# A division six cells behind its head, a supply that counts steps without matmuls, and an output bias on VectorE

## The chip, the cores and the metric

The kernel runs on one core of a Trainium2 chip. The metric is the device time of one execution in microseconds (us), taken as the median of several runs. Engines are named as in the profile: PE is TensorE's matmul, PEld its weight load, DVE is VectorE, ACT ScalarE, POOL GpSimd, and SP (SPq for its queue) the engine that issues most of the transfers.

## The reference

Two transformer blocks run one after the other on x, which is 2 batches of 1024 rows by 256 columns in fp32. The context has 64 tokens a batch. Layer 0 ends with a mixture of 8 experts of which each row takes two; layer 1 masks part of the context and ends with a plain feed-forward part.

```python
# layer 0
q = _ln(latents, sa_ln_g, sa_ln_b)
x = latents + _mha(q, q, sa_in_w, sa_in_b, sa_out_w, sa_out_b)      # 16 heads of 16
qc = _ln(x, ca_q_ln_g, ca_q_ln_b)
kv = _ln(tokens, ca_kv_ln_g, ca_kv_ln_b)
x = x + _mha(qc, kv, ca_in_w, ca_in_b, ca_out_w, ca_out_b)
x = _fuse_moe(x, ...)      # top 2 of 8, gates by softmax, gelu(h @ fc1) @ fc2
# layer 1
x = x + softmax(q @ k.T * SCALE) @ v @ sa_proj        # on layer_norm(x)
x = x + softmax(q @ kc.T * SCALE + bias) @ vc @ ca_proj
x = x + (gelu(layer_norm(x) @ fc1_w.T + fc1_b) @ fc2_w.T + fc2_b)
```

## The kernel before

**Cells.** The self-attention of a layer is a loop over 128 cells (lines 949 to 986), 64 for each batch. Eight cells in a row belong to one group of four heads, and a cell is one of that group's 8 blocks of 128 keys. The loop works on two cells at once. For the cell itself it makes four score matmuls of 128 x 512 ("b", L807), whose exponentials ScalarE takes (L813). For the cell that is LEAD = 10 ahead it makes four score matmuls of the other orientation ("a", L796), whose maxima over the keys VectorE takes (L803). Each matmul fills one of the eight PSUM banks; they go out in two slots of four, two of each kind. So in cells 0 to 117 VectorE has four maxima a cell, and in the last ten cells none; `maxima[0]` holds which of the two is the case, and helper() (L305) returns GpSimd while maxima are made and VectorE otherwise.

**Products.** Every even cell, the weights of the two cells before are multiplied with the values (L858, eight matmuls a cell), ScalarE copies the bank to a part buffer (L870; there are two), and helper() adds it to the head's sum (L871). If an odd cell has placed little other work (`most > 2.0`, L984), its predecessor's product is issued in the odd cell alone; then the even cell behind it has only its own half.

**Maxima to queries.** When the maxima of a head group are complete, VectorE gathers them (L831) and largest(h) transposes them on PE (L704) and subtracts them from the queries (L706). This is a task that may run at the next cell, and it is forced in the one after, before the first "b" scores of that head group.

**End of a head group.** finish() (L710) runs three cells behind a group's last. For each pair of groups it sends sums by DMA, takes reciprocals one cell later (L488), spreads them through a DMA two cells later (by_s<-turns, L493), and divides the result by them with helper() at `late` cells (L499, `late = 3 + maxima[0]`). At late + 1 the output projection (L428, added to x at L436) is made a task, and with it the cross-attention of those 512 rows; in layer 0 then their dispatch to the experts (L1294), in layer 1 the normalization of the feed-forward part (L1787).

**Filler.** All work beside the cells is a task of a Stream (L131): a generator that issues some instructions and yields a cost. A positive cost is the time of PE that they take; zero or a negative one means that only other engines work and that the task should wait so long. Stream.step (L152) picks the able task that is due first and repeats until a step has a positive cost. The loop keeps a debt, `owed`, to which each cell adds Stream.pace (at least 2.5 in layer 0 and 1.1 in layer 1, more where tasks have a due cell), and in a cell calls step until the debt is under 0.6 or `most`, which begins at 3.0, is spent:

```python
            owed = min(owed, 3.0) + max(stream.pace(cell), 0.0 if has_a else 2.0)
...
            most = 3.0
            while owed > 0.6 and most > 0.0:
                cost = stream.step(cell)
                if cost is None:
                    break
                owed -= cost
                most -= cost
```

A task that yielded a zero or negative cost can't run again in the same cell. What is left when the cells end is issued by Stream.rest (L178), by rank. In layer 0 the experts' slots follow (L1644, L1674, with indirect stores on POOL's queue); in layer 1 the rest of the cross-attention and the feed-forward part (L1804, L1816).

**Cross-attention and bias.** The cross-attention of 512 rows has scores (L1101, L1131), maxima (L1151), a subtraction of them by POOL while maxima are made and else by VectorE (L1152), exponentials (L1171), sums and reciprocals (L1190, L1199) and products with a division (L1205, L1212). add_bias (L417) adds a row of 256 to x: the self-attention's output bias before the blocks of a batch are used, the cross-attention's (layer 0), and the bias of the last feed-forward matrix (layer 1, L1793). All of it ran on GpSimd (L420). Each engine works its instructions off in the order in which the program issues them.

Of the kernel before, what the change touches and what calls it, by code (L numbers as in the profile page):

```python
# [45 lines left out]
ALU = mybir.AluOpType  # L46
# [4 lines left out]
P = 128  # L51
B, S, D, H, DH = 2, 1024, 256, 16, 16
# [78 lines left out]
class Stream:  # L131


    def __init__(self, rate):
        self.tasks, self.made, self.rate = [], set(), rate

    def add(self, steps, cost, **k):
        self.tasks.append(Task(steps, cost, **k))

# [12 lines left out]
    def step(self, cell):  # L152
        while True:
            able = [t for t in self.tasks if t.first <= cell and self.made.issuperset(t.after)]
            if not able:
                return None
            cost = self.advance(min(able, key=lambda t: (t.last, -t.rank)), cell)
            if cost and cost > 0.0:
                return cost

    def pace(self, cell):

# [39 lines left out]
def two_blocks(  # L202
# [16 lines left out]
    nc = tc.nc  # L219
# [83 lines left out]
    maxima = [True]  # L303

    def helper():  # L305

        return nc.gpsimd if maxima[0] else nc.vector
# [109 lines left out]
    def add_bias(first, nt, bias):  # L417
        for t0 in range(first, first + nt, 2):
            xb = x_sb[:, t0 : t0 + 2, :]
            nc.gpsimd.tensor_tensor(xb, xb, bias.unsqueeze(1).to_broadcast([P, 2, D]), ALU.add)  # L420

    def project_task(src, w, first, t0, n):

# [45 lines left out]
    def send(o, n, half, sm):  # L469


        nc.sync.dma_start(out=sm[64 * half : 64 * (half + 1), :], in_=o[DH::32, :])
        nc.sync.dma_start(out=whole[n, P * half : P * (half + 1), :], in_=o)

    def gather(n, dst):

        nc.sync.dma_start(
            out=dst, in_=whole[n].rearrange("(h r) q -> h r q", r=32)[:, :DH, :]
        )

    def next_heads():

        npair[0] += 1
        return npair[0] - 1

    def invert(n, sm):

        nc.vector.reciprocal(sm, sm)  # L488
        nc.sync.dma_start(out=turns[n], in_=sm)

    def spread_out(n, by):

        nc.sync.dma_start(  # L493
            out=by,
            in_=turns[n].rearrange("(h c) q -> h (c q)", h=8).unsqueeze(1).to_broadcast([8, DH, 512]),
        )

    def divide(dst, by):
        helper().tensor_tensor(dst, dst, by, ALU.mult)  # L499
# [17 lines left out]
    def self_attention(layer, tail, heads, arrive, extra, when_ready, beside=None):  # L517
# [27 lines left out]
        stream, later = Stream(RATE[layer]), {}  # L545
        maxima[0] = True

        def at_cell(cell, go):
            later.setdefault(cell, []).append(go)
# [143 lines left out]
        def need_heads(h):  # L693
            if h % 2 == 0:
                if h // 4 % 2 == 0 and h > 0:
                    stream.until(("K", h))
                stream.until(("Q", h))
# [12 lines left out]
        def finish(h, cell):  # L710


            b, qh, g = h // 8, h // 4 % 2, h % 4
            if g == 0:
                ot[b, qh] = opool.tile([P, 2, 512], F32, tag="ot", name=f"ot_{names}{b}{qh}")
            if layer == 0 and h >= 8 * B - 2:

                if g == 3:
                    stream.add(
                        side_by_side([acc.pop(h - 1), acc.pop(h)], ot[b, qh][:, 1, :]), 2.0,  # L720
                        mark="compact", rank=80,
                    )
                    project(b, qh, ["compact"])
                return
            if g % 2 == 0:
                sm = small.tile([P, 32], F32, tag="sums", name=f"sums_{names}{h}")
                sums[g // 2] = next_heads(), sm
            n, sm = sums[g // 2]
            dst = ot[b, qh][:, g // 2, :]
            send(acc.pop(h), n, g % 2, sm)  # L730
            if g % 2 == 1:
                by = opool.tile([P, 512], F32, tag="by", name=f"by_{names}{h}", bufs=1)
                gather(n, dst)
                at_cell(cell + 1, lambda: invert(n, sm))
                at_cell(cell + 2, lambda: spread_out(n, by))

                late = 3 + maxima[0]
                at_cell(cell + late, lambda: divide(dst, by))
                if g == 3:
                    at_cell(cell + late + 1, lambda: project(b, qh))  # L740

        def side_by_side(parts, dst):

            i, o = bank()
            j, s = bank()
            for half, part in enumerate(parts):
                nc.tensor.matmul(
                    o[64 * half : 64 * (half + 1), :], lhsT=picks[:, O_ROWS : O_ROWS + 64],
                    rhs=part, start=True, stop=True,
                )  # L750
            for half, part in enumerate(parts):
                for c in range(4):
                    nc.tensor.matmul(
                        s[32 * c : 32 * (c + 1), :P],
                        lhsT=picks[:, O_PART + 32 * half : O_PART + 32 * (half + 1)],
                        rhs=part[:, c * P : (c + 1) * P],
                        start=(half == 0),
                        stop=(half == 1),
                    )
            inv = small.tile([P, P], F32, tag="inv", name=f"inv_{names}", bufs=1)  # L760
            nc.vector.reciprocal(inv, s[:, :P])
            nc.scalar.copy(dst, o)
            free.extend((j, i))
            yield 1.5
            yield -1.6
            i, by = bank()
            for c in range(4):
                nc.tensor.matmul(
                    by[:, c * P : (c + 1) * P],
                    lhsT=picks[:, O_HEAD + c * P : O_HEAD + (c + 1) * P],  # L770
                    rhs=inv, start=True, stop=True,
                )
            nc.vector.tensor_tensor(dst, dst, by, ALU.mult)
            free.append(i)
            yield 0.55
            yield -1.0

        def project(b, qh, after=()):
            def go():
                for t0 in range(0, 4, 2):  # L780
                    yield from project_task(ot[b, qh], w, b * TB + 4 * qh + t0, t0, 2)
                when_ready(b, qh, stream, now[0])

            stream.add(go(), 4.0, last=now[0] + 4, rank=60, after=after)
# [45 lines left out]
        def collect(h):  # L830
            nc.vector.tensor_reduce(spread[h % 2][:, :, DH::32], mx.pop(h), AX.X, ALU.max)  # L831
# [8 lines left out]
        def slot(parts):  # L840

            drains = [score(*p) for p in parts]
            for i, drain in drains[::2] + drains[1::2] if len(parts) == 4 else drains:
                drain()
                free.append(i)
# [103 lines left out]
        for cell in range(ncell + 2):  # L949
            now[0] = cell  # L950
            ahead = cell + LEAD
            if ahead < ncell and ahead % 16 == 0:
                need_heads(ahead // 8)
            has_a, has_b = ahead < ncell, cell < ncell
            maxima[0] = has_a
            a = [("a", ahead, j) for j in (2, 3, 0, 1)] if has_a else []
            s = [("b", cell, j) for j in range(4)] if has_b else []
            if has_a:
                slot(s[:2] + a[:2])
                slot(s[2:] + a[2:])  # L960
            elif has_b:
                slot(s)
            if ahead % 8 == 7 and has_a:
                h = ahead // 8
                collect(h)
                stream.add(largest(h), 0.75, first=cell + 1, last=cell + 2, mark=("QB", h))
            if (cell + 1) % 8 == 0 and cell + 1 < ncell:
                stream.until(("QB", (cell + 1) // 8))
            for go in later.pop(cell, []):
                go()  # L970
            owed = min(owed, 3.0) + max(stream.pace(cell), 0.0 if has_a else 2.0)
            if cell >= 2 and cell % 2 == 0:
                product([c for c in (cell - 2, cell - 1) if c not in alone])
                if owed < 2.5:
                    continue
# [8 lines that stand above are left out]
            if cell % 2 == 1 and most > 2.0 and cell < ncell:  # L984
                alone.add(cell - 1)
                product([cell - 1])
# [945 lines left out]
    stream, later, _, _ = block(0, tail)  # L1932
# [47 lines left out]
    with ExitStack() as tail:  # L1980
        stream, later, made, ready = block(1, tail, heads, beside)
# [155 lines left out]
```

## Time and profile before

| what | before |
|---|---|
| median of 3 runs | 1632.26 us (1632.18 to 1632.59) |
| profiled execution | 1638.78 us, span 1637.0 us, mean granted TensorE clock 0.978 |
| cells of layer 0 | 52.5 to 592.6 us |
| cells of layer 1 | 965.0 to 1474.1 us, its cell 118 at 1438.8 us |
| maxima on VectorE, L803 | 1024 of 682 ns, 634.7 us busy |
| exponentials, L813 | 1024 of 609 ns |
| addition L871 on POOL, on DVE | 141 of 1272 ns, 14 of 694 ns |
| copies L870 on ACT | 155 of 598 ns |
| division L499 on POOL | 12 of 1271 ns, 59.6 us idle before ten of them, until by_s landed |
| add_bias, L420, on POOL | 16 for output biases of 1272 ns, 8 for the last bias of 1295 ns |
| L1152 on POOL, on DVE | 38 of 1054 ns, 26 of 692 ns |

A row of groups shows the line, the engine, the operation, its tiles with their shapes, how often it ran, then busy us and the mean ns of one, then the engine's idle time before such instructions and what ended it. A row of the timeline shows the start, the duration, the engine and the operation, and in brackets the idle time before it and what it waited for. A row of the windows shows the busy time of PE, PEld, DVE, ACT and POOL in a stretch with their instructions, then the granted clock of TensorE, the share of DMA and GB/s.

### The profile page before, as it was taken

How to read it: one execution, taken by the hardware profiler on the slowest of the kernel's cores; microseconds unless marked ns; L12 is line 12 of the kernel's file. 1: busy time of each engine (PE TensorE's matmuls, PEld its weight loads, DVE VectorE, ACT ScalarE, POOL GpSimd, SP SyncE). 2: the span in 40 equal slices, each digit the busy share in tenths (PEclk: the TensorE clock that was granted, in tenths of full speed). 3: DMA queues.
4: the chain of work that ended last, by engine and by line, in shares of the span. 5: the costliest groups of instructions: out<-in, count | busy, mean ns of one | idle time of the engine just before them, and what ended most of it. 6: DMA issues, size and time to landing. Idle time of an engine off the chain costs nothing.

```text
span 1637.0 us, 28319 instructions
## 1 busy us (share of the span) xinstructions
PE 1591.4 (97%) x10710; PEld 882.4 (54%) x10710; DVE 982.7 (60%) x2094; ACT 912.9 (56%) x1767; POOL 410.6 (25%) x545
## 2 busy tenths in 40 slices
PE   7999999999999998999999999999999999999998
PEld 3433444544543446878888753344344435446766
DVE  5796767687678647421113457876867867855400
ACT  3486767676765753333322327876776676674321
POOL 2243423134235202141112032411321323321010
PEclk9898999999999998999999999999999999999999
DMA  5234311101000105276567321000110002000000
GB/s 157 111 132 171 131 27 34 28 21 47 14 21 34 53 30 188 78 270 216 176 204 241 91 65 33 21 27 17 38 39 19 25 14 83 15 14 21 14 13 26
DMA packets 55751, 121.07 MB, mean 74 GB/s; under 512 B 12218, under 2 KB 26428, under 8 KB 55228
## 3 DMA queue, kind: packets, MB, share of 16 engines
q1 hardware_dynamic: 51772, 109.07, 20.9%
q0 software_dynamic: 3456, 9.51, 1.6%
q8 instruction: 86, 1.41, 0.4%
q10 hardware_dynamic: 384, 0.66, 0.2%
q14 instruction: 53, 0.43, 0.1%
HBM read 71.68 MB, written 38.88 MB: 68 GB/s over the span
## 4 chain that ended last, share of the span: by engine, by line
PE 89%; DVE 7%; issue 1%; ACT 1%; DMA 1%; another core or an unknown queue 1%; POOL 0%; SPq 0%; DVEq 0%; POOLq 0%; ACTq 0%
PE banks L807 16%; PE banks L796 15%; PE banks L858 14%; PE banks L1674 8%; PE banks L1644 8%; PE banks L626 4%; PE banks L428 3%; PE banks L1816 3%; PE banks L1804 3%; DVE mx_s L803 3%; PE banks L1131 2%; PE banks L596 2%; PE banks L1167 2%; PE banks L360 2%; PE banks L1101 2%
## 5 line engine op out<-in xcount | busy, mean ns | idle before, releaser
L803 DVE TENSOR_REDUCE mx_s<-banks 128x1 f32<-128x512 f32 x1024 | 634.7, 682 | 221.2 <-PE banks L796 214.9
L813 ACT ACTIVATE pt_s<-banks 128x512 f32<-128x512 f32 x1024 | 532.6, 609 | 155.5 <-PE banks L796 124.4
L796 PE MATMUL banks<-KS,QS 16*128 16x512 f32 x2048 | 539.5, 633 | 4.0 <-ACT part_s L870 1.6
L807 PE MATMUL banks<-qb_s,KS 32*128 32x512 f32 x2048 | 519.2, 623 | 6.6 <-DVE qb_s L706 3.7
L871 POOL TENSOR_TENSOR acc_s<-acc_s,part_s 128x512 f32<-128x512 f32 x141 | 179.4, 1272 | 442.2 <-ACT part_s L870 441.5
L807 PEld LDWEIGHTS banks<-qb_s,KS 32*128 32x128 f32 x2048 | 181.3, 187 | 178.6 <-DVE mx_s L803 104.4
L858 PE MATMUL banks<-pt_s,v_s 128*20 128x512 f32 x2048 | 264.1, 607 | 1.5 <-DVE mx_s L803 1.0
L796 PEld LDWEIGHTS banks<-KS,QS 16*128 16x128 f32 x2048 | 201.1, 186 | 76.8 <-issue 37.3
L1674 PE MATMUL banks<-w_slot,h_s 128*128 128x256 f32 x640 | 145.4, 383 | 3.0 <-ACT h_s L1650 3.0
L858 PEld LDWEIGHTS banks<-pt_s,v_s 128*20 128x20 f32 x2048 | 43.2, 99 | 187.5 <-ACT pt_s L813 132.1
L1674 PEld LDWEIGHTS banks<-w_slot,h_s 128*128 128x128 f32 x640 | 121.7, 192 | 23.5 <-ACT h_s L1650 3.4
L870 ACT COPY part_s<-banks 128x512 f32<-128x512 f32 x155 | 92.7, 598 | 65.1 <-PE banks L858 54.5
L1683 DVE SCALAR_TENSOR_TENSOR ys<-banks,gate,b 128x256 f32<-128x256 f32 x40 | 19.3, 483 | 174.2 <-PE banks L1674 166.3
L1650 ACT ACTIVATE h_s<-banks,w_slot 128x256 f32<-128x256 f32 x104 | 43.7, 471 | 111.6 <-issue 65.3
L1689 POOL DMA_INDIRECT results<-ys,to x40 | 38.7, 967 | 255.0 <-DVE ys L1683 211.2
L1644 PE MATMUL banks<-xsT,w_slot 128*128 128x256 f32 x416 | 95.6, 381 | 0.7 <-ACT xsT L367 0.7
L1644 PEld LDWEIGHTS banks<-xsT,w_slot 128*128 128x128 f32 x416 | 77.4, 190 | 14.9 <-DVE mx_s L803 2.3
L1152 POOL TENSOR_TENSOR sc_c<-sc_c,mx_c 128x512 f32<-128x512 f32 x38 | 40.0, 1054 | 102.4 <-DVE mx_c L1151 102.4
L626 PE MATMUL banks<-xT_s,w_att 128*128 128x512 f32 x128 | 64.7, 642 | 0.0
L1807 ACT ACTIVATE h_f<-banks,w_ff 128x512 f32<-128x512 f32 x32 | 22.0, 687 | 73.9 <-PE banks L1804 73.9
L1650 ACT ACTIVATE h_s<-banks,spare 128x256 f32<-128x256 f32 x56 | 23.4, 471 | 62.8 <-issue 31.3
L1816 PE MATMUL banks<-w_ff,h_f 128*128 128x256 f32 x256 | 57.3, 380 | 0.0
(269 smaller groups left out, 1651.4 us busy)
## 6 DMA issues: line engine op xcount, KB each, us to landing
w_slot<-in_ff_w_dram SPq DMA_DIRECT2D x40, 576.0 KB
sorted_rows<-fill SPq DMA_DIRECT2D x36, 520.0 KB
w_slot<-in_ff_w_dram SPq DMA_DIRECT2D x26, 514.0 KB
whole<-acc_s SPq DMA_DIRECT2D x30, 256.0 KB
spare<-in_ff_w_dram SPq DMA_DIRECT2D x14, 514.0 KB
xs<-sorted_rows SPq DMA_DIRECT2D x20, 260.0 KB
y<-results SPq DMA_DIRECT2D x16, 256.0 KB
QS<-stq_s SPq DMA_DIRECT2D x124, 32.0 KB
```

The source lines that it names most:

```text
L626: nc.tensor.matmul(p, lhsT=w[:, at + k * D + pair * P : at + k * D + (pair + 1) * P], rhs=xT[b][:, k, blk * 512 : (blk + 1) * 512], start= ...
L796: nc.tensor.matmul(sc, lhsT=QS[h % 4][r, qc * P : (qc + 1) * P], rhs=K[r, kh * 512 : (kh + 1) * 512], start=True, stop=True,)
L803: return i, lambda: nc.vector.tensor_reduce(mx[h][:, qc, j, kh : kh + 1], sc, AX.X, ALU.max)
L807: nc.tensor.matmul(sc, lhsT=K[r, n * P : (n + 1) * P], rhs=QB[h][r, :], start=True, stop=True)
L813: nc.scalar.activation(pt, sc, AF.Exp, scale=SCALE)
L858: nc.tensor.matmul(o[32 * j : 32 * j + VW, :], lhsT=V[b][:, cell % 8, 4 * g + j, :], rhs=exps.pop((cell, j)), start=(cell == cells[0]), st ...
L870: nc.scalar.copy(part, o)
L871: helper().tensor_tensor(acc[h], acc[h], part, ALU.add)
L1644: nc.tensor.matmul(ph[:, n, :], lhsT=w[:, at : at + P], rhs=xT[:, k, :], start=(k == 0), stop=(k == 1),)
L1650: nc.scalar.activation(h1[:, f, :], ph[:, n, :], AF.Gelu, bias=w[:, W_B1 + f : W_B1 + f + 1])
L1674: nc.tensor.matmul(py, lhsT=h1[:, f, h * P : (h + 1) * P], rhs=w[:, f * D : (f + 1) * D], start=(f == 0), stop=(f == 7),)
L1816: nc.tensor.matmul(py[:, n, :], lhsT=h1[:, f, t * P : (t + 1) * P], rhs=w2[:, f * D : (f + 1) * D], start=(f == 0), stop=(f == 7),)
```

## The change

Three things are changed. A Stream has a number `others`, which the loop sets to 0.8 in the cells that make maxima and to 0 in the last ten; a step then returns at least that number as its cost, also where the step had a zero or negative cost, and so a step that issued no matmul now ends the search and is taken off both `owed` and `most`. A task's own remaining cost, from which the pace is worked out, is not touched, and Stream.rest does not use the number. Second, `late` is 6 while maxima are made and 3 otherwise, so the division stands six cells behind finish() and the projection seven. Third, add_bias uses helper() instead of GpSimd, so it is VectorE's where no maxima are made.

```diff
@@ class Stream
         self.tasks, self.made, self.rate = [], set(), rate
 
+        self.others = 0.0
+
@@ step
             cost = self.advance(min(able, key=lambda t: (t.last, -t.rank)), cell)
-            if cost and cost > 0.0:
-                return cost
+            if cost is not None and max(cost, self.others) > 0.0:
+                return max(cost, self.others)
@@ add_bias
-            nc.gpsimd.tensor_tensor(xb, xb, bias.unsqueeze(1).to_broadcast([P, 2, D]), ALU.add)
+            helper().tensor_tensor(xb, xb, bias.unsqueeze(1).to_broadcast([P, 2, D]), ALU.add)
@@ finish
-                late = 3 + maxima[0]
+                late = 6 if maxima[0] else 3
                 at_cell(cell + late, lambda: divide(dst, by))
                 if g == 3:
                     at_cell(cell + late + 1, lambda: project(b, qh))
@@ the loop over cells
             maxima[0] = has_a
+            stream.others = 0.8 if has_a else 0.0
```

## The prediction

> **What bounds the kernel now.** I read the page's totals, the groups, the chain that ended last, a table of four stretches (attention of layer 0; experts; layer 1's cells 0 to 117; the rest), the timeline around the largest gaps, then the waits.
>
> ```profile
> PE 1591.4 (97%) x10710; PEld 882.4 (54%) x10710; DVE 982.7 (60%) x2094; ACT 912.9 (56%) x1767; POOL 410.6 (25%) x545
> PE 89%; DVE 7%; issue 1%; ACT 1%; DMA 1%; another core or an unknown queue 1%; POOL 0%; SPq 0%; DVEq 0%; POOLq 0%; ACTq 0%
> L803 DVE TENSOR_REDUCE mx_s<-banks 128x1 f32<-128x512 f32 x1024 | 634.7, 682 | 221.2 <-PE banks L796 214.9
> 52.50:592.60 540.10, 532.62 (x3911) 235.99 (x3912) 390.79 (x753) 371.33 (x718) 174.02 (x227) 0.96 0.17 57
> 592.60:965.00 372.40, 359.40 (x1820) 292.20 (x1820) 146.81 (x522) 122.04 (x264) 67.38 (x70) 0.97 0.50 165
> 965.00:1438.80 473.80, 466.55 (x3638) 208.46 (x3638) 347.43 (x608) 330.82 (x632) 135.85 (x171) 0.99 0.12 34
> 1438.80:1637.00 198.20, 190.72 (x1181) 123.85 (x1180) 63.64 (x133) 74.56 (x130) 17.23 (x48) 1.00 0.05 17
> ```
>
> TensorE is the bound nearly everywhere, and the matmuls do not change. So a gain can only be stall between them or throttled clock. Columns: span, PE, PEld, DVE, ACT, POOL busy, clock. The clock is 0.96 in layer 0 and 0.99 to 1.00 in layer 1: layer 0 loses about 540 x 0.04 = 22 us to half-clock stretches, inside a busy time that looks full.
>
> I took a cell's duration less its matmuls at full speed as its stall. Layer 0's cells 0 to 117 hold 60.7 us of stall (9.5 at start-up), layer 1's 26.7 us (5.9 at start-up), 0.23 a cell. Two places in layer 0 stand out, cells 23 and 24 (7.8 us) and 111 and 112 (9.2 us):
>
> ```profile
> 135.69 1.27 POOL L499 TENSOR_TENSOR ot_s<-ot_s,by_s 128x512 f32<-128x512 f32 x1 [7.63 <-DMA by_s<-turns]
> 136.91 3.95 POOL L871 TENSOR_TENSOR acc_s<-acc_s,part_s 128x512 f32<-128x512 f32 x3
> 138.21 0.59 ACT L870 COPY part_s<-banks 128x512 f32<-128x512 f32 x1 [3.31 <-POOL acc_s L871]
> 138.84 1.70 PE L796 MATMUL banks<-KS,QS 16*128 16x512 f32 x4 [1.62 <-ACT part_s L870]
> ```
> ```profile
> 135.20:150.50 15.30, 13.68 (x53) 3.57 (x52) 5.97 (x10) 5.90 (x11) 7.54 (x6) 0.67 0.37 147
> 520.70:539.80 19.10, 17.87 (x65) 5.86 (x64) 12.77 (x27) 7.91 (x15) 10.67 (x10) 0.73 0.11 38
> ```
>
> The division L499 waits in POOL's queue for its transfer, three additions wait behind it, the copy L870 waits for a part buffer, and PE for a bank. The clock is then 0.67. At cell 111 VectorE runs the search's and normalization's small operations between maxima; the clock is 0.73.
>
> [...] The trace agrees on the half (a pair of L807 takes 1.06 us from 143 on, 0.59 before) but gaps of only 1.6 us (before 139.3) or 1.0 us (before 402) were followed by it, while four gaps of 0.90 us were not. [...] here L871 takes 1272 ns on POOL and 694 on VectorE, 1.8x.
>
> **The change, part by part.**
>
> *1. Division at +6 while maxima are made.* The matmuls, the division and its 1.27 us stay; it moves two cells, 2 x 2.93 = 5.9 us (a bare cell runs 1047.26 to 1050.19), and issues no DMA. The projection it is tied to moves too: 8 matmuls in 2 steps, with an addition L436 of 0.69 us each on VectorE. At cell 23 POOL would reach the division at cell 24, about 138, after the transfer's landing at 135.69: the 7.63 us wait goes, and with it the 7.8 us of cells 23 and 24, which include about 10.2 x 0.5 = 5.1 us of half clock. What is late next is the ordinary limit of a cell. Elsewhere the division's waits (59.6 us in all) hold only an idle POOL: nothing. Value -7.5, ends -8 and -2 (a transfer late by more cells, or half clock from another gap).
>
> *2. Steps of other engines counted at 0.8 in layer 0.* The order of the changed kernel's instructions has the same filler matmuls there (155.2 against 151.6 us by cell 126), later by 2 to 8 cells and spread: dispatch in cells 75 to 83 and 104 to 116, one step a cell, the search at 114 to 119. Addressable stall, from the cells: 44-47 0.9; 67-70 1.4; 75-80 5.8; 82-84 6.3; 97-102 2.75; 105-108 5.4; 111-112 9.2; 114-116 1.0: together 32.7. A cell has 2.93 - 2.48 = 0.45 us of VectorE to spare beside its maxima: cells 106 and 107 held 2.2 to 2.5 us of small operations and stalled 1.82 and 2.38, so one step of 1.0 us a cell leaves about 0.55. What I expect in their place: 75-81 four steps and two bare cells 3.4 to 3.8 (3.4), 108-112 the same (3.8), 69 and 99 2.0, search in 114-119 1.0, half clock again in some (half a chance of 4) 2.0, the unexplained 1 us "issue" gap of cell 83 with the half clock behind it (half a chance of 5.5) 2.75, and bare odd cells: 15.0. Bare odd cells are new: 9, 45, 57, 89 (and 75, 79, 109, 111, in the sums above) have no product and no filler: 1.93 us of matmuls (2.85 less 0.92 of a product) against 2.48 us of maxima. PE then waits for VectorE to free a bank, with the next cell's scores and so ScalarE's exponentials queued behind. The trace has no such cell; behind odd cells with some 0.5 us of filler the stall is 0.43 to 0.58 (cell 54 of layer 1: 5.56 us for 5.00). Bounds: 0.5 and 1.0 (0.5 + the missing 0.5); value 0.8, 4 x 0.8 = 3.2, so 18.2 remain. Gain 32.7 - 18.2 = 14.5, ends 4 and 24.
>
> *3. The same in layer 1.* Filler in cells 0 to 117 falls from 136.3 to 104.2 us: 32 us of matmuls, mostly cross-attention, move behind cell 118. PE-bound work moved into a PE-bound stretch costs nothing; its surroundings do. Six bare odd cells (9, 51, 77, 91, 101, 113): 6 x 0.8 = 4.8. The query maxima L704/L706 are forced at the last moment in 9 heads instead of 5; such a cell shows this wait:
>
> ```profile
> 1152.04 0.68 DVE L706 TENSOR_TENSOR qb_s<-QS,banks 128x512 f32<-128x512 f32 x1
> 1152.87 0.70 PE L807 MATMUL banks<-qb_s,KS 32*128 32x512 f32 x2 [0.90 <-DVE qb_s L706]
> ```
>
> That is stall 0.98 a cell: 4 x 0.8 = +3.2. Fewer cross steps inside cells give back 3, uneven rest +1: together +6. Ends -3 and +20 (below). In the rest, 30 us more cross work lies in a PE that is 96% busy there; its chain uses VectorE (L1152 692 ns against POOL's 1054), 12 such operations move to it in the changed order. I take +3 for holes where L1199 (958 ns) or L1152 is waited for, ends -1 and +10. The last forward part keeps about 10.4 us of matmuls as cover for the last normalization against 12: nothing.
>
> *4. Bias by VectorE without maxima.* Ten of 24 L420 (POOL 1.27 us) become VectorE's, about 0.69 us as for L871: the eight of the forward part and two behind layer 0's cells. Behind cell 118 VectorE is 32% busy (63.64 of 198.20) and matmuls fill 96%: that is the cover. Nothing; without the cover 10 x 0.69 = +7 at most, -3 if POOL's latency was waited for.
>
> *5. Queues.* The dispatch's indirect stores on POOL move with their steps, 2 to 8 cells; the SP order differs in 28 places, spreads of QS and KS. Experts begin after the cells as before. Their own holes (7.08 us at 627, 5.65 at 697, 6.54 at 720, beside weight loads) may shift: 0, ends -4 and +4. The copies L870 fall from 155 to 139 and the additions with them: POOL and ACT are not the bound, nothing.
>
> Sum: -7.5 - 14.5 + 6 + 3 = -13. Since no trace shows the bare cell and half clock comes and goes, I keep 10 of it, i.e. 3 us for throttling in new places. Profiled execution: 1638.78 (span 1637.0 and 1.8 around it), so 1628.8; the median of the runs is 6.5 lower, 1632.26, giving 1622.3.
>
> **Rivals.** *Layer 1's cells run dry (slower).* VectorE's maxima alone are 118 x 2.48 = 293 of 474 us, and taking 32 us of matmuls from those cells saves 32 only if the cells stay PE-bound; behind cell 118 the 32 us are paid in full. For: the bare cells and the late L706. Against: the mean cell keeps (474 - 32)/118 = 3.7 us, above 2.48. If the stall doubles from 0.23 a cell (+27 us) against the gain of 22 in layer 0 and +3 behind, 1632.3 + 8 = 1640. It decides from (22 - 3)/118 = 0.16 us a cell.
>
> *The stalls only move (no change).* Small VectorE operations still stand between maxima, one cell later[...]. For: half clock followed gaps as short as 0.6 to 1.0 us. Against: a step a cell is what the cell's slack of VectorE (2.93 - 2.48) can nearly hold. Layer 0 then gains only 9: 1632.3 - 9 + 9 = 1632.
>
> *Only the division acts.* -7.5 and layer 1's bare cells undone by its saved steps, +1 behind: 1626.
>
> **How the numbers follow.** Forecast 0.45 (own range 1610 to 1629), only the division 0.13, no change 0.14, slower 0.28. The measurement tells 0.2% (3.3 us) from no change: faster is below 1629.0. Faster 0.58, same 0.14, slower 0.28. The range leaves out 0.1 below (both gains at their ends, -32 + 6 + 3 less some: 1608) and 0.1 above 1642.
>
> **What would show it.** In the changed profile: no POOL wait of 7 us for by_s and no clock of 0.67 near 140; the stretch of cells 0 to 117 of layer 0 shorter by 15 to 25 us, its clock 0.98; layer 1's same cells shorter by about 26 (32 - 6), the rest longer by 33; L870 139 times; cells such as 51 and 91 at 2.5 us and more with DVE gapless. It is wrong if layer 1's cells shorten by less than 15, if layer 0's clock stays at 0.96, or if the experts' stretch differs by over 4 us.

## The result and the profile after

The changed kernel takes 1652.29 us (median of 14 runs) against 1632.42 us of before: it is slower, ratio 1.0096 with a 95% interval of 1.0081 to 1.0111, some 15.7 us. The medians lie further apart, 19.9 us, and the means 16.5 us; what follows is taken from ratios. The forecast was 1622 us, its range ended at 1642 us.

Executions of one kernel lie 3 to 21 us apart here (11 us for the kernel before, 18 for the changed one), so small effects are taken from the ratios, and the traces, each of one execution, serve for the places. The profiled execution after took 1649.77 us (span 1648.0, clock 0.981), 11.0 us above that of before. These are the page's totals, chain and clock row after:

```profile
PE 1595.4 (97%) x10710; PEld 893.1 (54%) x10710; DVE 991.2 (60%) x2128; ACT 904.8 (55%) x1743; POOL 362.6 (22%) x495
PEclk9899999999998998999999999999999999999999
PE 90%; DVE 6%; DMA 1%; issue 1%; another core or an unknown queue 1%; ACT 0%; SPq 0%; POOL 0%; DVEq 0%; POOLq 0%; ACTq 0%
```

The matmuls are the same 10710, and the kernel is as full as it was: shares do not show a loss. The four stretches that the prediction was built on do. This is the table of windows after, with layer 0's cells, the experts, layer 1's cells 0 to 117, and the rest:

```profile
51.40:588.90 537.50, 531.71 (x3893) 239.13 (x3891) 388.81 (x750) 364.08 (x703) 156.16 (x213) 0.97 0.17 57
588.90:964.00 375.10, 359.07 (x1843) 293.28 (x1840) 146.77 (x528) 118.23 (x259) 65.07 (x68) 0.98 0.49 164
964.00:1418.10 454.10, 442.44 (x3348) 192.74 (x3348) 334.56 (x582) 316.52 (x604) 115.36 (x143) 1.00 0.12 35
1418.10:1648.00 229.90, 220.60 (x1469) 146.16 (x1468) 87.66 (x191) 91.77 (x153) 10.07 (x43) 0.98 0.05 15
```

| stretch | before | after | difference | forecast |
|---|---|---|---|---|
| lead-in | 52.5 | 51.4 | -1.1 | 0 |
| layer 0's cells | 540.1 | 537.5 | -2.6 | -22 |
| experts | 372.4 | 375.1 | +2.7 | 0 |
| layer 1's cells 0 to 117 | 473.8 | 454.1 | -19.7 | -26 |
| rest of layer 1 | 198.2 | 229.9 | +31.7 | +33 |

The two large numbers of layer 1 came near the forecast, but together they are +12.0 instead of the +9 of the prediction's sum (its terms, 32 us moved and 3 of stall, would make the last row +35), and layer 0's gain is missing almost whole. Cells 0 to 117 of layer 0 alone are 7.6 us shorter (505.6 to 498.0), 6.8 of it less loss by clock, but cells 118 to 127 are 4.8 us longer. The first place to look at is the division at cell 23. This is the timeline after, at the same place as before (L501 is the division, L873 the addition, L872 the copy, L798 a score):

```profile
136.72 1.27 POOL L501 TENSOR_TENSOR ot_s<-ot_s,by_s 128x512 f32<-128x512 f32 x1 [7.52 <-DMA by_s<-turns]
137.94 3.95 POOL L873 TENSOR_TENSOR acc_s<-acc_s,part_s 128x512 f32<-128x512 f32 x3
139.23 0.58 ACT L872 COPY part_s<-banks 128x512 f32<-128x512 f32 x1 [3.20 <-POOL acc_s L873]
139.87 1.13 PE L798 MATMUL banks<-KS,QS 16*128 16x512 f32 x4 [1.51 <-ACT part_s L872]
```

The wait has not moved: 7.52 us, three additions behind it, a copy, a gap on PE. (The half clock behind it took 3.4 us in this execution, from 141.1 on, and 10.2 us in that of before.) The division is issued two cells later in the program, yet POOL takes it up where it did before. The kernel writes the order out by hand for PE, DVE, ACT and SP only (the `manual_schedule` in its head); POOL's order is left to the framework's scheduler, and in both traces the division stands behind the same two additions of the next head group. The sentence ahead of the prediction, that each engine works in the order of the program, is wrong for POOL. The prediction used the changed kernel's order of instructions, but placed the division in POOL's queue as the program issues it.

For what follows, time was split in each trace into idle time of PE (no matmul on it), loss by clock (duration times 1 less the granted clock) and the remainder. Here "half clock" is a stretch at a granted clock of 0.5; in all traces such stretches last a multiple of 3.41 us (3.41 to 13.65 in that of before), unless the execution ends in them. Since a trace is one execution, the loss by clock was also averaged over all executions of a kernel, each of which has its span and mean clock on record; that table stands behind the experiments.

### The profile page after: what moved, and what is told of

The parts are those of the page before. It is cut to its first block, busy times and chain, and to the rows that moved or that the text cites. A ratio compares the mean times of both kernels' runs of the same rounds, so it can differ in the third digit from the quotient of the medians.

```text
span 1648.0 us, 28264 instructions
## 1 busy us (share of the span) xinstructions
PE 1595.4 (97%) x10710; PEld 893.1 (54%) x10710; DVE 991.2 (60%) x2128; ACT 904.8 (55%) x1743; POOL 362.6 (22%) x495
## 4 chain that ended last, share of the span: by engine, by line
PE 90%; DVE 6%; DMA 1%; issue 1%; another core or an unknown queue 1%; ACT 0%; SPq 0%; POOL 0%; DVEq 0%; POOLq 0%; ACTq 0%
PE banks L809 17%; PE banks L798 15%; PE banks L860 14%; PE banks L1677 8%; PE banks L1647 8%; PE banks L628 4%; PE banks L430 3%; PE banks L1807 3%; PE banks L1819 3%; DVE mx_s L805 2%; PE banks L1134 2%; PE banks L598 2%; PE banks L1170 2%; PE banks L1104 2%; PE banks L362 1%
## 5 line engine op out<-in xcount | busy, mean ns | idle before, releaser
L798 PE MATMUL banks<-KS,QS 16*128 16x512 f32 x2048 | 537.9, 629 | 2.4 <-ACT part_s L872 1.5
L809 PE MATMUL banks<-qb_s,KS 32*128 32x512 f32 x2048 | 525.5, 620 | 13.0 <-DVE qb_s L708 7.3
L809 PEld LDWEIGHTS banks<-qb_s,KS 32*128 32x128 f32 x2048 | 187.0, 186 | 184.9 <-DVE mx_s L805 105.4
L873 POOL TENSOR_TENSOR acc_s<-acc_s,part_s 128x512 f32<-128x512 f32 x127 | 160.9, 1267 | 433.6 <-ACT part_s L872 432.7
L798 PEld LDWEIGHTS banks<-KS,QS 16*128 16x128 f32 x2048 | 205.8, 185 | 75.0 <-issue 37.0
L872 ACT COPY part_s<-banks 128x512 f32<-128x512 f32 x139 | 82.8, 596 | 73.1 <-PE banks L860 61.9
L1807 PE MATMUL banks<-hT_f,w_ff 128*128 128x512 f32 x128 | 57.1, 594 | 0.0
```

The source lines that it names most:

```text
L798: nc.tensor.matmul(sc, lhsT=QS[h % 4][r, qc * P : (qc + 1) * P], rhs=K[r, kh * 512 : (kh + 1) * 512], start=True, stop=True,)
L809: nc.tensor.matmul(sc, lhsT=K[r, n * P : (n + 1) * P], rhs=QB[h][r, :], start=True, stop=True)
L872: nc.scalar.copy(part, o)
L873: helper().tensor_tensor(acc[h], acc[h], part, ALU.add)
L1807: nc.tensor.matmul(ph, lhsT=w1[:, at : at + P], rhs=hT[:, k, :], start=(k == 0), stop=(k == 1))
```

## The experiments

Ratios are against runs of the kernel before on the same chip, with 95% intervals. First, each part alone.

**Steps counted, alone.** In the kernel before:

```diff
+            if cost is not None and max(cost, self.others) > 0.0:
+                return max(cost, self.others)
...
+            stream.others = 0.8 if has_a else 0.0
```

> The kernel before with only the counted steps (0.8 in cells with maxima). If the supply is the cause, this alone is slower by 0.5 to 1.0% (8 to 16 us): layer 1's cells 0 to 117 lose about 25 us of filler to the end and gain only 19. If the projection moved to +7 is the cause, this is within 0.2% of before.

Measured: 1.0086 (1.0057 to 1.0116). The supply is a cause of that size. Its trace shows layer 1 beginning 11.7 us earlier than before and the time behind layer 1's last cell 27 us longer, so the two layers had to be taken apart.

**Division and projection later, alone.**

```diff
-                late = 3 + maxima[0]
+                late = 6 if maxima[0] else 3
```

> The kernel before with only late = 6. In the changed kernel's trace POOL still takes up the first division behind the same additions as before, so theory: its wait of 7.5 us at cell 23 stays and the time is within 0.3% of before. Rival: the projection and with it cross-attention and dispatch come two to three cells later, the end of layer 0's cells gets fuller, and it costs 4 to 8 us. The prediction's own claim was -7.5 us.

Measured: 1.0053 (1.0033 to 1.0072), some 8.7 us. My theory of "no change" fell; the rival is right that the later projection costs. The division's wait is there as before. These are POOL's rows of its timeline:

```profile
138.81 1.27 POOL L499 TENSOR_TENSOR ot_s<-ot_s,by_s 128x512 f32<-128x512 f32 x1 [7.18 <-DMA by_s<-turns]
140.03 3.96 POOL L871 TENSOR_TENSOR acc_s<-acc_s,part_s 128x512 f32<-128x512 f32 x3
```

**Bias alone.**

```diff
-            nc.gpsimd.tensor_tensor(xb, xb, bias.unsqueeze(1).to_broadcast([P, 2, D]), ALU.add)
+            helper().tensor_tensor(xb, xb, bias.unsqueeze(1).to_broadcast([P, 2, D]), ALU.add)
```

> The kernel before with only add_bias by helper(). Theory: within 0.2% (ten additions of 0.69 us on a VectorE that is a third busy). Rival: they stand before the normalization or the search in VectorE's queue, and cost up to 7 us.

Measured: 0.9992 (0.9974 to 1.0009). No difference that can be told.

**Late, and the division held.** A VectorE operation on one column of `by` ties POOL's division to the place in the program:

```diff
     def divide(dst, by):
+        if maxima[0]:
+            nc.vector.tensor_scalar(by[:, 0:1], by[:, 0:1], 1.0, None, ALU.mult)
         helper().tensor_tensor(dst, dst, by, ALU.mult)
```

> The kernel before with late = 6, and a VectorE operation on one column of by ahead of each such division, so that POOL can't take the division up earlier: it then stands behind three or four more additions. Theory: the wait of 7.5 us for by_s and the half clock behind cell 23 are gone, 4 to 8 us below the kernel with late = 6 alone. Rival: the time of cell 23 was no loss that stays, and both are alike.

Measured: 1.0008 (0.9991 to 1.0025), 0.45% or 7.3 us below late alone. These are rows of this kernel's timeline (L500 is the added operation):

```profile
138.57 1.27 POOL L873 TENSOR_TENSOR acc_s<-acc_s,part_s 128x512 f32<-128x512 f32 x1 [2.24 <-DMA sorted_rows<-fill]
141.29 0.14 DVE L500 TENSOR_SCALAR by_s<-by_s 128x1 f32<-128x1 f32 x1
141.51 1.26 POOL L501 TENSOR_TENSOR ot_s<-ot_s,by_s 128x512 f32<-128x512 f32 x1 [1.67 <-DVE by_s L500]
```

The additions now run ahead of the division, the wait of 7 us for the transfer is gone (the 1.67 us left are for the added operation; PE has no gap in cells 16 to 31), and so is the half clock that ran from 139.3 to 149.5 us before. Cells 16 to 31 take 51.4 us for the same matmuls that took 59.1 before.

**Steps counted in layer 0 only.** (`late` and bias as before.)

```diff
+            stream.others = 0.8 if has_a and layer == 0 else 0.0
```

> The kernel before with the steps counted at 0.8 in layer 0 only. Theory: layer 0 gains what is gained at all by the supply (9 to 12 us up to the start of layer 1 in the profile of the supply alone), so 0.992 to 0.997 of before. Rival: layer 0's stalls only move and half clock follows them, 0.998 to 1.002.

Measured: 0.9988 (0.9968 to 1.0008). The rival's value, though the interval just reaches the theory's 0.997. In the trace PE's idle time in layer 0's cells 0 to 117 falls from 7.3 to 4.9 us, and the loss by clock is 22.2 us against 20.5: the gaps are smaller and half clock stays in this execution. It begins elsewhere, at 408.7 us for 10.2 us and at 518.0 for 6.8. Over all executions the picture is another one, as the table below shows.

**Steps counted in layer 1 only.**

```diff
+            stream.others = 0.8 if has_a and layer == 1 else 0.0
```

> The kernel before with the steps counted at 0.8 in layer 1 only. Theory: this is the whole loss, 1.008 to 1.014 of before (13 to 23 us): cells 0 to 117 some 20 us shorter, the rest some 35 longer. Rival: only the bare cells and late L706 cost, 8 us, 1.004 to 1.006.

Measured: 1.0107 (1.0085 to 1.0129), some 17.5 us, as the theory had it; the rival's 1.006 lies outside. This alone is as large as the whole loss.

**The same with the work kept in the cells.**

```diff
-RATE = (2.5, 1.1)
+RATE = (2.5, 1.7)
```

> As the supply in layer 1 only, with layer 1's rate 1.7 instead of 1.1, so that cells 0 to 117 hold as much filler as before (136 us) with steps still spread and six bare odd cells. If the loss is that work is pushed behind cell 118, the time is back at before, 0.998 to 1.002; if it is the bare and uneven cells, it stays above 1.005.

Measured: 0.9998 (0.9979 to 1.0017). Five bare odd cells are there and steps are counted, and the time is that of before: with as much filler inside, counting costs nothing that can be told. (In the traces cells 0 to 117 hold 828 matmul records of filler, against 820 before.)

**The work pushed out without counting.** The kernel before with a lower rate:

```diff
-RATE = (2.5, 1.1)
+RATE = (2.5, 0.8)
```

> The kernel before with layer 1's rate 0.8 instead of 1.1 and no counted steps: 25 us of filler leave cells 0 to 117 for the rest, as in the changed kernel, but no bare odd cells come. If pushing work behind the cells costs by itself (half clock behind runs of small matmuls, waits in the last cross-attentions), 1.004 to 1.010. If the counting of steps is what costs, 0.998 to 1.002.

Measured: 1.0042 (1.0028 to 1.0057), 6.9 us: pushing work out costs by itself, here 248 of the 820 records of filler. It is less than half of the 1.0107 for pushing out 288 with counting, so the two together cost more than pushing alone.

**The first pair's division held, steps counted in layer 0.** The second pair's division and its projection stay at +4 (that division is tied there as well):

```diff
-                late = 3 + maxima[0]
+                late = (6 if g == 1 else 4) if maxima[0] else 3
...
+            nc.vector.tensor_scalar(by[:, 0:1], by[:, 0:1], 1.0, None, ALU.mult)
...
+            stream.others = 0.8 if has_a and layer == 0 else 0.0
```

> The kernel before with the supply counted in layer 0 only, the division of a first pair at +6 and held there by a VectorE operation on a column of by, that of a second pair, with its projection, at +4 as before. Theory: the wait at cell 23 goes (7 us) and layer 0's gain by the supply stays (9), 0.988 to 0.994 of before. Rival: the two gains are of the same stalls, 0.995.

Measured: 0.9946 (0.9924 to 0.9967), median 1627.07 us: faster than both kernels, but the rival's value (the interval holds the theory's slow end, 0.994, too).

**The same with more filler in layer 1.**

```diff
-RATE = (2.5, 1.1)
+RATE = (2.5, 1.5)
```

> As the kernel with the first pair's division held at +6 and the supply counted in layer 0 only, with layer 1's rate 1.5 instead of 1.1: 10 us more filler in layer 1's cells 0 to 117. If less work behind the cells is worth what more of it costs, 3 to 6 us below that kernel: 0.990 to 0.993 of before. Rival: layer 1's rest is PE-bound without loss already, and it stays at 0.9946.

Measured: 0.9983 (0.9973 to 0.9994), worse than without. My expectation fell. The trace shows the loss by clock in layer 1's cells 0 to 117 at 11.9 us, against 0.0 without: half clock from 1402.0 us for 10.2 us and from 1419.0 for 6.8, behind gaps of 1.65 and 2.19 us on PE. Here more filler in cells with maxima is a loss as well.

**The changed kernel with each division held**, edit as above.

> The changed kernel with each division held behind a VectorE operation on a column of by at +6. The wait of 7.5 us at cell 23 goes, with 3.4 us of half clock behind it: 4 to 7 us below the changed kernel, 1.005 to 1.008 of before. Rival: held divisions at other heads delay projections, no gain, 1.0096.

Measured: 1.0067 (1.0043 to 1.0090), 0.29% below the changed kernel. Some 4.8 us, as expected, but the intervals overlap.

**The changed kernel without layer 1's counting.**

```diff
-            stream.others = 0.8 if has_a else 0.0
+            stream.others = 0.8 if has_a and layer == 0 else 0.0
```

> The changed kernel with the steps counted in layer 0 only. Layer 1's counting alone cost 1.07%; if that is the whole of the loss here too, the time is at or just under before, 0.996 to 1.001. If the later projections (late alone 1.0053) add to it unhindered, 1.003 to 1.006.

Measured: 1.0035 (1.0020 to 1.0051). It is the second case: the late projection's cost stands here too. Against layer 0's counting alone (0.9988), late and bias add 0.47%, as late alone did (0.53%).

**The small matmuls apart.** Why is pushed work dear, where PE has no gaps to speak of? In the trace with layer 1's counting, half clock begins behind cell 118 at 1439.2 us for 3.4 us and at 1497.2 for 10.2. This is PE's timeline at the second (L1125 adds the mask, weights of one row, L1134 is the cross score, weights of 32 rows, 128 columns each, L1170 a transpose):

```profile
1496.25 0.39 PE L1134 MATMUL banks<-kbd,q_c 32*128 32x128 f32 x4
1496.47 0.39 PE L1125 MATMUL banks<-mask_i,ones 1*128 1x128 f32 x4
1496.69 0.39 PE L1134 MATMUL banks<-kbd,q_c 32*128 32x128 f32 x4
1497.01 0.96 PE L362 MATMUL banks<-ident,xn_f 128*128 128x128 f32 x4
1497.76 1.91 PE L1170 MATMUL banks<-ident,sc_c 128*128 128x128 f32 x8
1499.61 0.80 PE L1125 MATMUL banks<-mask_i,ones 1*128 1x128 f32 x4
1500.20 0.64 PE L1134 MATMUL banks<-kbd,q_c 32*128 32x128 f32 x4
```

There is no idle time: a row of 64 records of small matmuls ran from 1493.58 to 1497.08 us, and then everything is slower (0.64 for 0.39 us). The kernel before has such a row as well, from 1519.15 to 1522.65 us, and there the clock stays. These are the windows of the row and of the 3.41 us behind it, first before, then with layer 1's counting (the clock is the third number from the end):

```profile
1519.15:1522.65 3.50, 3.50 (x66) 3.38 (x65) 1.32 (x3) 0.69 (x1) 0.00 (x0) 1.00 0.02 5
1522.65:1526.06 3.41, 3.41 (x29) 2.98 (x30) 3.31 (x7) 0.96 (x1) 0.00 (x0) 1.00 0.00 0
```
```profile
1493.58:1497.08 3.50, 3.50 (x66) 3.38 (x66) 1.39 (x3) 0.69 (x1) 0.00 (x0) 1.00 0.00 0
1497.08:1500.49 3.41, 3.41 (x21) 3.05 (x22) 3.31 (x6) 2.45 (x4) 0.00 (x0) 0.52 0.02 5
```

To test whether the row matters, one wait of 0.1 us lets another task step in between the two halves of that row:

```diff
-            (SC, 0, 0, None),
+            (SC, 0, 0, -0.1),
```

> The kernel with the steps counted in layer 1 only, and a wait of 0.1 between the first two score steps of a cross-attention where no maxima are made, so that two or four dense matmuls of the feed-forward part stand between the two runs of 32 small ones. If half clock behind a run of small matmuls is the larger part, the stretches of half clock behind cell 118 (13.6 us at 1439 and 1497) go and the time falls by 4 to 8 us, to 1.003 to 1.008. If waits are what costs, it stays at 1.0107.

Measured: 1.0057 (1.0039 to 1.0075), 0.50% or 8.2 us below the kernel without the wait, whose interval it doesn't touch. PE's timeline in this kernel:

```profile
1485.56 0.39 PE L1134 MATMUL banks<-kbd,q_c 32*128 32x128 f32 x4
1485.87 1.99 PE L1807 MATMUL banks<-hT_f,w_ff 128*128 128x512 f32 x4
1487.79 0.49 PE L1125 MATMUL banks<-mask_i,ones 1*128 1x128 f32 x4
...
1489.45 0.39 PE L1134 MATMUL banks<-kbd,q_c 32*128 32x128 f32 x4
1489.77 1.99 PE L1819 MATMUL banks<-w_ff,h_f 128*128 128x256 f32 x8
1491.60 1.04 PE L1170 MATMUL banks<-ident,sc_c 128*128 128x128 f32 x8
```

Dense matmuls of the feed-forward part stand in the row, and the transposes behind it take 1.04 us, not 1.91. The windows of 1460 to 1560 us, first without, then with the scores apart:

```profile
1460.00:1560.00 100.00, 96.42 (x747) 69.97 (x747) 51.61 (x127) 41.81 (x66) 11.22 (x32) 0.95 0.04 14
```
```profile
1460.00:1560.00 100.00, 98.10 (x737) 68.35 (x736) 53.15 (x127) 40.71 (x62) 10.98 (x32) 1.00 0.05 15
```

From cell 118 to the last matmul the loss by clock falls from 6.8 us (5.1 of it directly behind the row) to 0.0, and PE's idle time from 4.7 to 2.4 us. The edit moves other steps there too, and the idle time may be theirs; the clock's share is the larger.

**The fastest kernel with the same wait.**

> The fastest kernel so far (first pair's division held at +6, steps counted in layer 0 only) with the same wait between the scores. Its rest shows no half clock to be removed, so within 0.3% of 0.9946; faster only if single stretches of 3.4 us come and go there between executions.

Measured: 0.9938 (0.9914 to 0.9962), median 1627.18 us. Not told apart from 0.9946; it is the fastest version of this study beside that one. Parting the scores gains nothing that can be told here, as expected: in the trace without it no half clock stands behind the rows.

**The division of a first pair held, alone.** As the faster kernel, with

```diff
-            stream.others = 0.8 if has_a and layer == 0 else 0.0
+            stream.others = 0.0
```

> The kernel before with only the first pair's division at +6, held there, the second pair's at +4. If the gain of the fastest kernel is this wait of 7.5 us and the half clock behind it, 0.994 to 0.996. If layer 0's counted steps are part of it, 0.997 to 0.999.

Measured: 0.9954 (0.9936 to 0.9972), 7.5 us below before. So the faster kernels owe their gain to this division; layer 0's counting adds nothing that can be told (0.9946). (The second pair's division is tied too, at its old place; no run parts the two.)

**All executions.** The loss by clock of an execution is its span times 1 less its mean clock; all else is the rest of its span. This table has the means over all executions of each kernel, less those of the kernel before in the same comparison (33.8 us by clock and 1600.7 of all else over its 130 executions, which also serve for the changed kernel). The first column is good to some 1 to 2 us, the second to some 0.5 to 1.

| kernel | by clock, us | all else, us |
|---|---|---|
| the changed kernel | -0.7 | +15.2 |
| steps counted, both layers | +0.3 | +12.0 |
| late alone | +7.5 | +2.0 |
| bias alone | -1.4 | -0.2 |
| late, divisions held | +3.4 | -2.5 |
| first pair's division held | -4.6 | -2.5 |
| the same, layer 0 counted | -9.3 | +0.5 |
| the same, more filler in layer 1 | -2.2 | +0.2 |
| layer 0 counted | -3.7 | +2.0 |
| layer 1 counted | +7.9 | +10.3 |
| low rate in layer 1 | +6.5 | +2.6 |
| layer 1 counted, scores apart | +2.7 | +6.7 |

The changed kernel loses no more by the clock than the kernel before: its loss is all else.

## Why the prediction was wrong, point by point

**The division (-7.5): the step failed, its size was right.** "At cell 23 POOL would reach the division at cell 24, about 138, after the transfer's landing": it did not, since POOL's queue isn't in the program's order (its wait is 7.52 us after, 7.63 before). Held in its place the division gives -7.5 us (0.9954) without and -7.3 us (1.0053 to 1.0008) with the later projection.

**The projection, put at nothing: a failed step.** The text named it and priced no effect of it. Two pairs of kernels that differ in it, and in the second pair's division to which it is bound, agree: without held divisions 1.0053 against 1, with held divisions 1.0008 against 0.9954, each 0.53 to 0.54%, 8.7 to 8.8 us. By the table nearly all of it is lost by the clock, 7.5 and 8.0 us. Where is shown in part only. In the trace of late alone half clock begins at 1478.6 and 1540.1 us, each time behind such a row of small matmuls as is shown above and for 3.4 us; that is 2 x 3.4 x 0.5 = 3.4 us which the kernel before does not lose, and with the division held the two stretches are there as well (1456.3 and 1517.8). For layer 0 the two traces differ too much in clock (a loss of 37.5 us and of 18.8; the first is of the slowest of eleven executions) to place the rest; it stays open.

**Layer 0's counted steps (-14.5): mis-sized.** It measured 0.9988, -2 us, and -1.3 us between the two kernels with the held division. By the table counting does reduce the half clock, by 3.7 and 4.7 us in these two comparisons, but all else grows by 2.0 and 3.0 us. The estimate took a stall's half clock as part of the stall: remove the gap, and both go. The traces show that smaller gaps can be followed by it too, and larger ones not: in the kernel before it came 0.5 us behind a gap of 0.64 us (at 523.9) and did not come behind one of 1.37 us (at 1448.6). In the changed kernel VectorE's step of 1.28 us (L1347) and the small operations behind it hold up the maxima and leave PE idle for 1.38 us at 508.0, and then the clock is halved for 6.8 us; the cell takes 10.6 us for 4.4 us of matmuls. "The stalls only move" was a rival at 0.14, and its value for layer 0 is about what was measured.

**Bare odd cells (0.8 each): slightly low, and not by VectorE.** Cell 52 of layer 1, behind a bare cell, takes 4.81 us, and cell 50 with the same matmuls 3.78 us, a loss of 1.03 us; the cells behind layer 1's five others take 4.81 to 4.85 us. The timeline after shows ScalarE without a break across the two cells, and the weight load waits for it:

```profile
1162.48 4.24 ACT L815 ACTIVATE pt_s<-banks 128x512 f32<-128x512 f32 x8 [0.50 <-PE banks L798]
1162.51 2.48 DVE L805 TENSOR_REDUCE mx_s<-banks 128x1 f32<-128x512 f32 x4 [1.29 <-PE banks L798]
1163.13 0.41 PEld L809 LDWEIGHTS banks<-qb_s,KS 32*128 32x128 f32 x4 [0.70 <-ACT pt_s L815]
```

The exponentials' banks, not the maxima's, came free last here.

**Layer 1 (+6 +3): the failed step is "PE-bound work moved into a PE-bound stretch costs nothing".** It measured +17.5 us alone. Counting with the work kept inside costs nothing that can be told (0.9998), pushing alone 6.9 us, both 17.5. The table parts the 17.5: all else is +10.3 us, near the 6 + 3 of the forecast, and the clock +7.9 us, near the 17.5 - 9 = 8.5 us that were missed. The prediction had a clock of 1.00 behind cell 118 and took it for granted. Parting the scores gives back 8.2 us, by the table 5.2 by the clock and 3.6 of all else, so parting the rows of small matmuls removes a large part of the clock's share; that they are all of it is not shown. Nor are the rows new: the kernel before has two of 58 and 64 records behind cell 118, at 1458.1 and 1519.2 us, and was not struck; with layer 1's counting there are three, and one was. With the scores apart PE is still idle 11.6 us in layer 1's cells 0 to 117, against 7.2 before: in mechanism this is the slower rival, "layer 1's cells run dry". The prediction has half clock only behind gaps; with layer 1's counting the row at 1493.58 us has none, and the clock behind it was 0.52.

**Bias (0): right.** 0.9992. **Experts (0, ends -4 and +4): right in size,** +2.7 us in the profile. (The "holes" of 7.08, 5.65 and 6.54 us are links of the chain that ended last: PE itself is idle 3.74 us behind 631.5, 2.96 us behind 702.7 and not at all from 720 to 727.) **Copies L870:** 139, as forecast; no run prices them.

**The sum.** The four steps missed by 7.5 (division), 8.7 (projection), 12.5 (layer 0) and 8.5 us (layer 1), 37 in all, where the sum of -13 was missed by 29. Late 1.0053, layer 0's counting 0.9988, layer 1's 1.0107 and bias 0.9992 would give 1.0140 if they added; the changed kernel is 1.0096 (1.0081 to 1.0111), and with four intervals of about 0.2% each the sum is uncertain by some 0.4%. The table shows which half does not add: all else of the four parts sums to 14.1 us, against 15.2 in the changed kernel, their loss by clock to 10.3, against -0.7. So the parts' clock does not carry over to the whole; why it is less there stays open.

## What to carry to other kernels

Before pricing a step that is moved, look up where its engine takes it up: POOL, whose order a scheduler makes, did not follow the program here (it waited 7.52 us at the old place), and a tie to an operation on an ordered engine put the step where it was meant to be (-7.5 us). Where TensorE is the bound, split its time into idle time, clock and the remainder; a busy share of 97% hides both a clock of 0.96 and its causes. One trace is one execution: where the clock matters, average it over many. Filler is not the same everywhere: pushed to the end of this kernel it cost more than its own time (6.9 us more at the low rate), and dense matmuls set between runs of small ones gave back 0.5% in one kernel and nothing in another.

## What was not expected of the hardware

Half clock came without any idle time. Behind cell 118 of layer 1 the 17 traces hold 33 rows of 58 or 64 records of matmuls with weights of 1 and 32 rows and 128 columns, 3.1 to 4.0 us long, in which PE has no gap (none in the two kernels with the scores apart). In ten traces half clock begins in the last 1.2 us of such a row or up to 0.6 us behind it, 12 times in all; 21 rows, the two of the kernel before among them, were not followed by it.

The two kinds differ in where the row lies. In each trace the stretches of half clock begin whole multiples of 3.413 us apart: in the kernel before at 26.63, 53.94, 139.27 and 402.10 us, which is 8, 25 and 77 times that. In the changed kernel the first is at 25.07 us, so these places, counted from the start, differ from trace to trace. With each trace cut from its first such place into steps of 3.413 us, each of the 12 rows that were followed covered 0.83 to 0.99 of one step, each of the 21 others 0.54 to 0.80. In the kernel before the two rows covered 0.63 and 0.74; in the changed kernel the one that was followed, from 1492.61 us, covered 0.97, and the two others 0.60 and 0.54. Late alone, struck twice, and the kernel before, spared, have the same two rows and differ in this. It was found in the traces afterwards, and no run was made to test it.

By the profile's record PE is busy throughout these rows (3.51 of 3.51 us in the one from 1492.61 us), and half clock came behind this one all the same (0.50 over the next 3.41 us). What it is in these rows, no run here separates.
